# A decoder layer in float32: x transposed in blocks by VectorE and through DRAM, and an altered order of stages in the plan

## The chip, the cores and the metric

The kernel runs on one core of a Trainium2 chip. The core has a matrix engine (TensorE, PE in the profile, with its weight loads listed as PEld), a vector engine (VectorE, DVE), a scalar engine (ScalarE, ACT), GpSimd (POOL) and a queue engine (SyncE, SP) that issues transfers (DMAs). The engines run side by side and wait for one another by semaphores. The metric is the device time of one execution in microseconds (us), taken as the median of several runs.

## The reference

All data are float32. `x` has 16 batches of 512 tokens with 256 channels, and `ctx_1024` has 16 batches of 64 context tokens. Three sublayers follow one another, each added to its input and normalised over the channels:

```python
# 1. linear self-attention, 16 heads of 16 channels, K = 2
q  = x + x @ Wq + bq
ks = x + x @ Wk[k] + bk[k];  vs = x + x @ Wv[k] + bv[k]        # k = 0, 1
states[k] = einsum('bhnd,bhne->bhde', ks / 32, vs / 32)
out = einsum('bhnd,bhde->bhne', q, prod(states))               # no softmax
out = (layernorm(out) * ln_g + ln_b) @ Wo + bo
# 2. cross-attention to 64 context tokens, 16 heads of 64
out = softmax(q k^T * SCALE, masked) v @ Wout.T + b_out
# 3. mixture of experts: 8 experts, 256 -> 1024 -> 256, capacity 1024 tokens each
w = softmax(x @ router_w.T + router_b)
out[token] += w[token, e] * (relu(x[token] @ Wi[e]) @ Wo[e])   # first 1024 tokens with w > 0, per expert
```

With softmax weights nearly always above zero, each expert takes the first 1024 tokens, which are batches 0 and 1.

## The kernel before, in words

**Self-attention without ks and vs.** Because there is no softmax, the state of a batch needs only the Gram matrix of x (`x^T x`, 256x256) and the sums of x. `gram` (L550) loads x of one batch into `gx` with a column of ones (`load_gram_x`, L293: tokens on partitions, token t*128 + p in partition p), multiplies it with itself into `ps_g` and copies the result to `g`. The order of the tokens makes no difference to it. `self_attention` (L614) then multiplies `g` with the weights (`ps_gk` L629, `ps_s` L641), folds the state into one matrix `m` (`ps_m` L670), and applies it to x: `ps_o` (L687) needs x with channels on partitions, which is `xT`. Before the change `xT` is made from `xt`, a second load of x, by `transposed` (L227): per half of the channels four TensorE transposes of 128x128 into one PSUM bank (L233), and one copy out of it by `evac` (L182), in turn on ACT and DVE. Norm, a transpose of z (`zT`, which shares its one buffer with `xT`), the output product `ps_p` (L711), norm, and the transposed `x1T` follow.

**The other stages.** `context_keys` (L450), `output_weights` (L515) and `context_values` (L483) prepare keys and values of all batches once and store them in DRAM (`k_dram`, `vo_dram`). `cross_attention` (L765) per batch: a key product per pair of batches (`ps_kq` L751), scores `ps_sim` (L814), a softmax whose probabilities DVE transposes in 32x32 blocks (L804), and the product with the values `ps_x` (L834), for which `vo` comes from DRAM in 32 DMAs per batch. `routing` (L846) computes expert weights into `w_all`; the `experts` (L929, `ps_h` L946, `ps_e` L963) work on the first two batches, beside the attention of the others. `ranks` (L875) checks at the end whether later batches have tokens for an expert; the weights it lets through are written to `w_sel`, and a loop at the end of the kernel handles such batches. There are none here.

**The order.** The order of the instructions on PE, DVE, ACT and POOL is fixed by a planner: each stage is a generator, a `Stream`, that emits a few instructions at a time. `weave` (L1010) always advances the ready stream with the earliest planned time, where the time is that of `plan(at, span, total)`: start, length and PE work, so it moves on with the work done. `Model` (L28) estimates when each instruction would be done; `yield WAIT` makes a stream ready only when what it has emitted is done, `until(...)` waits for a condition. `in_order` (L1029) then ties the instructions of each of the four engines to that order. SP's queue, which issues all DMAs before the change, isn't tied by it. The constants are `SETUP = 115` and `STEP = 78` us, one step per batch. The Gram matrix of batch b >= 4 is planned at SETUP + (b - 4.8) STEP, the self-attention of b at SETUP + (b - 1) STEP, the cross-attention at SETUP + b STEP, routing one step later. The context stream (71 us of PE work, then 28 for the second half of the values) is planned from 5 us to about 200 us, and the experts from SETUP + 1.3 STEP on. The first four Gram matrices are planned within the first 40 us, and after the fourth the remaining weights are loaded.

## Time and profile before

| | us |
|---|---|
| median of 3 runs | 1384.72 (1383.49 to 1386.94) |
| the profiled execution | 1389.4 |
| its span | 1387.6 |
| granted TensorE clock, mean | 0.994 |
| DMA, share of 16 engines on SP's queue | 40.1% of the span, 151.98 MB |

The profile lists per engine the busy time in the span, then groups of instructions by source line: output tile, input tiles, shapes, count, busy time, mean time of one, and the idle time before them. A matmul in float32 is recorded as two instructions, a transpose as one. "L233" is line 233 of the kernel before. The chain follows the work that ended last backwards, always to what released it, so it tells what set the end. A table by stage gives the busy time of each engine in a stretch. In the middle of the run the steps of 78 us look alike.

### The profile page before, as it was taken

How to read it: one execution, taken by the hardware profiler on the slowest of the kernel's cores; microseconds unless marked ns; L12 is line 12 of the kernel's file. 1: busy time of each engine (PE TensorE's matmuls, PEld its weight loads, DVE VectorE, ACT ScalarE, POOL GpSimd, SP SyncE). 2: the span in 40 equal slices, each digit the busy share in tenths (PEclk: the TensorE clock that was granted, in tenths of full speed). 3: DMA queues.
4: the chain of work that ended last, by engine and by line, in shares of the span. 5: the costliest groups of instructions: out<-in, count | busy, mean ns of one | idle time of the engine just before them, and what ended most of it. 6: DMA issues, size and time to landing. Idle time of an engine off the chain costs nothing.

```text
span 1387.6 us, 24209 instructions
## 1 busy us (share of the span) xinstructions
PE 1365.9 (98%) x9630; PEld 1077.9 (78%) x9630; DVE 850.7 (61%) x1957; ACT 402.2 (29%) x912; POOL 203.7 (15%) x140
## 2 busy tenths in 40 slices
PE   8999999999999999999999999999999999999997
PEld 5766576877878787878878787878888787878686
DVE  2445848466584848475584848475665939484744
ACT  1134224132232314142233323142323323232322
POOL 0001112112020111112020112112020202111200
PEclk9999999999999999999999999999999999999999
DMA  8657775511515153522606053513334061505211
GB/s 260 203 136 191 189 195 163 142 32 42 145 53 150 46 142 106 127 77 52 181 24 164 31 142 106 126 62 77 110 95 123 16 187 46 147 26 126 91 56 40
DMA packets 98372, 153.57 MB, mean 111 GB/s; under 512 B 15560, under 2 KB 70096, under 8 KB 98256
## 3 DMA queue, kind: packets, MB, share of 16 engines
q1 hardware_dynamic: 98256, 151.98, 40.1%
q8 instruction: 78, 1.28, 0.4%
q14 instruction: 38, 0.31, 0.1%
HBM read 114.71 MB, written 37.22 MB: 109 GB/s over the span
## 4 chain that ended last, share of the span: by engine, by line
PE 89%; DVE 5%; DMA 2%; SPq 1%; ACT 1%; issue 1%; ACTq 0%; DVEq 0%
PE ps_x L834 16%; PE ps_sim L814 15%; PE ps_e L963 15%; PE ps_h L946 15%; PE ps_gk L629 4%; PE ps_p L711 4%; PE ps_o L687 3%; PE ps_kv L437 3%; PE ps_t L233 2%; PE ps_kq L751 2%; PE ps_vo L492 2%; PE ps_s L641 2%; PE ps_g L555 2%; PE ps_zt L700 1%; PE ps_m L670 1%; PE ps_g L560 1%
## 5 line engine op out<-in xcount | busy, mean ns | idle before, releaser
L946 PE MATMUL ps_h<-head_T,wi 128*128 128x256 f32 x1024 | 239.1, 379 | 0.0
L834 PE MATMUL ps_x<-vo,pT 32*128 32x264 f32 x4096 | 234.9, 384 | 3.9 <-DVE pT L804 3.7
L814 PE MATMUL ps_sim<-kq,x1T 128*128 128x512 f32 x512 | 235.0, 593 | 0.0
L834 PEld LDWEIGHTS ps_x<-vo,pT 32*128 32x128 f32 x4096 | 211.5, 186 | 26.1 <-issue 5.6
L946 PEld LDWEIGHTS ps_h<-head_T,wi 128*128 128x128 f32 x1024 | 193.4, 190 | 38.8 <-issue 13.0
L802 POOL TENSOR_TENSOR s<-s,sm 128x1024 f32<-128x1024 f32 x64 | 121.7, 1901 | 539.8 <-DVE sm L801 501.4
L841 DVE TENSOR_TENSOR x<-ps_x,x 128x264 f32<-128x264 f32 x64 | 23.2, 426 | 226.3 <-PE ps_x L834 226.3
L822 ACT ACTIVATE s<-s 128x512 f32<-128x512 f32 x128 | 80.7, 630 | 276.1 <-DVE s L821 276.0
L814 PEld LDWEIGHTS ps_sim<-kq,x1T 128*128 128x128 f32 x512 | 94.5, 190 | 83.2 <-issue 74.5
L820 DVE TENSOR_REDUCE mx<-ps_sim 128x8 f32<-128x512 f32 x128 | 86.1, 673 | 42.0 <-PE ps_sim L814 41.6
L821 DVE TENSOR_TENSOR s<-ps_sim,mx 128x512 f32<-128x512 f32 x128 | 88.5, 692 | 4.4
L725 POOL TENSOR_TENSOR x<-x,bout 128x1056 f32<-128x1056 f32 x16 | 38.7, 2420 | 320.7 <-ACT hT L952 172.6
L804 DVE STREAM_TRANSPOSE pT<-s 128x1024 f32<-128x1024 f32 x64 | 78.6, 1228 | 7.0 <-POOL s L802 7.0
L952 ACT ACTIVATE hT<-ps_h 128x256 f32<-128x256 f32 x128 | 46.9, 376 | 119.9 <-PE ps_h L946 119.8
L701 ACT ACTIVATE zT<-ps_zt,shift,gain 128x512 f32<-128x512 f32 x32 | 23.2, 775 | 189.5 <-PE ps_zt L700 189.5
L800 DVE TENSOR_REDUCE sm<-s 128x16 f32<-128x1024 f32 x64 | 77.1, 1204 | 0.4 <-ACT s L822 0.4
L261 ACT ACTIVATE rstd<-bn_mv,eps 128x4 f32<-128x4 f32 (+1 forms) x70 | 20.7, 295 | 159.5 <-DVE bn_mv L250 156.0
L267 ACT ACTIVATE x<-x,off,rstd 128x264 f32<-128x264 f32 (+1 forms) x112 | 58.3, 591 | 29.3 <-DVE off L265 29.3
L687 PE MATMUL ps_o<-m,xT 128*128 128x264 f32 x256 | 66.7, 387 | 0.0
L954 DVE TENSOR_SCALAR hT<-ps_h 128x256 f32<-128x256 f32 x128 | 52.2, 409 | 22.5 <-PE ps_h L946 22.3
L711 PE MATMUL ps_p<-wo,zT 128*128 128x264 f32 x256 | 63.1, 387 | 0.0
L629 PE MATMUL ps_gk<-wk,g 128*128 128x256 f32 x256 | 61.2, 382 | 0.0
(174 smaller groups left out, 1897.4 us busy)
## 6 DMA issues: line engine op xcount, KB each, us to landing
vo<-vo_dram SPq DMA_DIRECT2D x512, 132.0 KB, 4.2
vo_dram<-vst SPq DMA_DIRECT2D x128, 132.0 KB, 2.4
xt<-in_x_dram SPq DMA_DIRECT2D x16, 512.0 KB, 4.0
wi<-L_ffn_experts_inter_dram SPq DMA_DIRECT2D x8, 1024.0 KB, 5.3
gx<-in_x_dram SPq DMA_DIRECT2D x15, 512.0 KB, 4.2
x_rest<-x SPq DMA_DIRECT2D x14, 512.0 KB, 3.1
out_dram<-x SPq DMA_DIRECT2D x14, 512.0 KB, 2.9
kT<-k_dram SPq DMA_DIRECT2D x8, 512.0 KB, 3.3
```

The source lines that it names most:

```text
L629: nc.tensor.matmul(ps[:, :C], blk, wk[:, j, k, :], start=(j == 0), stop=(j == NC - 1))
L687: nc.tensor.matmul(ps[:, :CX], xT[:, cc, t * P:(t + 1) * P], m[:, cc, :], start=(cc == 0), stop=(cc == NC - 1))
L711: nc.tensor.matmul(ps[:, :CX], zT[:, cc, t * P:(t + 1) * P], wo[:, cc, :], start=(cc == 0), stop=(cc == NC - 1))
L802: nc.gpsimd.tensor_mul(s, s, sm.unsqueeze(2).to_broadcast([P, NH, J]))
L804: nc.vector.transpose(probsT[:, :, t, :], s.rearrange("p h (a j) -> p (h a) j", a=2))
L814: nc.tensor.matmul(ps, x1T[:, cc, t * P:(t + 1) * P], kq[:, cc, hf * 512:(hf + 1) * 512], start=(cc == 0), stop=(cc == NC - 1),)
L820: nc.vector.tensor_reduce(mx[:, hs], sim, AX.X, ALU.max)
L821: nc.vector.tensor_sub(s[:, hs, :], sim, mx[:, hs].unsqueeze(2).to_broadcast([P, 8, J]))
L822: nc.scalar.activation(s[:, hs, :], s[:, hs, :], AF.Exp, scale=SCALE)
L834: nc.tensor.matmul(ps[q][:, :CX], probsT[pq, blk].rearrange("p t i -> p (t i)"), vos[c][pq, i, :], start=(c == 0 and i == 0), stop=(c == 7 ...
L946: nc.tensor.matmul(ps[:, :TB], wi[:, cc, f * P:(f + 1) * P], head_T[b][:, cc, t0 * P:t0 * P + TB], start=(cc == 0), stop=(cc == NC - 1),)
L963: nc.tensor.matmul(ps[:, :C], hT[f][:, t * P:(t + 1) * P], wo_[:, f, :], start=(f == 0), stop=(f == NF - 1),)
```

## The change

For batches 1 to 15, TensorE no longer transposes x. `load_gram_x` loads `gx` in four DMAs of 32 partitions each, so that partition 32 i + j holds the tokens 128 i + 32 q + j. After the Gram matrix, `to_blocks` lets DVE transpose `gx` in 32x32 blocks (four instructions per batch) into `xb`. ACT's queue writes `xb` to a DRAM tile of the batch, `x_blocks`. At the start of the batch's self-attention, `from_blocks` reads it back in four DMAs on ACT's queue, each to 32 partitions of `xT`, where the blocks now stand as the full transpose. The layout of `xT` changes accordingly. Batch 0 still uses TensorE. The second load of x, `xt`, stays for the residual. The next `gx` is loaded after this instead of right after the Gram products, and the self-attention waits until its blocks are in DRAM, and before `ps_o` until `xT` is there.

In the plan, the first self-attention and the first cross-attention get the planned time 0, which makes them the most urgent whenever they are ready, and the later self-attentions move from b - 1 to b - 1.6 steps. The planner's model learns DMAs on ACT. `w_sel` is gone: `ranks` writes the weights of the later batches over `w_all`. Two small tiles keep one buffer.

```diff
@@ Model.run @@
-            if kind == "InstDMACopy":
+            if kind == "InstDMACopy" and engine == "Activation":
+                start = max(at, self.free.get(engine, 0.0))
+                self.free[engine] = start + 0.35
+                done = start + 5.0
+            elif kind == "InstDMACopy":
...
+                by = "SP" if kind == "InstDMACopy" else engine
+                self.used[n] = max(self.used.get(n, (0.0, None)), (done, by), key=lambda p: p[0])
...
@@ decoder_layer @@
-    w_sel = const.tile([P, NTT, E], FP, tag="w_sel", name="w_sel")
...
+    def to_blocks(src):
+        xb = wk1.tile([P, NT, NC, NT, 32], FP, tag="xb", name="xb")
+        for q in range(NT):
+            nc.vector.transpose(
+                xb[:, :, :, q, :].rearrange("p k c j -> p c k j"),
+                src[:, q, :C].rearrange("p (c k j) -> p c k j", c=NC, j=32),
+            )
+        return xb
+
+    def from_blocks(dst, there):
+        for k in range(NT):
+            nc.scalar.dma_start(
+                out=dst[k * 32:(k + 1) * 32].rearrange("i t c n -> i t (c n)"),
+                in_=there[:, :, k, :].rearrange("t i n -> i t n"),
+            )
...
-        def load_gram_x(b, eng=nc.sync, pieces=1):
+        def load_gram_x(b, eng=nc.sync, pieces=NT):
...
+                else:
+                    eng.dma_start(
+                        out=t[i * 32:(i + 1) * 32, :, :C],
+                        in_=x[b, i * P:(i + 1) * P, :].rearrange("(q j) c -> j q c", j=32),
+                    )
...
@@ gram @@
-            if b + 2 < B:
-                gram_x[b + 2] = load_gram_x(b + 2)
...
             grams[b] = g
+            if b > 0:
+                yield WAIT
+                xb = to_blocks(gx)
+                yield WAIT
+                x_blocks[b] = dram.tile([NT, 32, NT, NC * P], FP, tag=f"x_blocks{b}", name="x_blocks")
+                nc.scalar.dma_start(
+                    out=x_blocks[b].rearrange("t i k n -> (t i) (k n)"), in_=xb.rearrange("p k c q j -> p (k c q j)")
+                )
+            if b + 2 < B:
+                gram_x[b + 2] = load_gram_x(b + 2)
             yield WAIT
...
@@ self_attention @@
-            xT = wk1.tile([P, NC, S], FP, tag="xT", name="xT")
-            gks = []
+            xT = wk1.tile([P, NT, NC, P], FP, tag="xT", name="xT")
+            if b > 0:
+                from_blocks(xT, x_blocks.pop(b))
...
-            yield from until(lambda: made(xt))
-            transposed(xT, xt)
+            if b == 0:
+                yield from until(lambda: made(xt))
+                transposed(xT.rearrange("p t c n -> p c t n"), xt, lambda t: t)
             yield WAIT
...
+            yield from until(lambda: made(xT))
             z = wk1.tile([P, NT, CX], FP, tag="z", name="z")
...
-                        ps[:, :CX], xT[:, cc, t * P:(t + 1) * P], m[:, cc, :], start=(cc == 0), stop=(cc == NC - 1)
+                        ps[:, :CX], xT[:, t, cc], m[:, cc, :], start=(cc == 0), stop=(cc == NC - 1)
...
@@ ranks @@
-            nc.vector.scalar_tensor_tensor(w_sel, rank, float(CAP), w_all, ALU.is_lt, ALU.mult)
+            rest = slice(HEAD_B * NT, NTT)
+            nc.vector.scalar_tensor_tensor(
+                w_all[:, rest], rank[:, rest], float(CAP), w_all[:, rest], ALU.is_lt, ALU.mult
+            )
...
@@ all_self_attention @@
-                self_st.plan(SETUP + (b - 1) * STEP, STEP, 16.5)
-                yield from until(lambda: b in grams and sums[b // QB][1] and "rb" in cs and made(grams[b], sums[b // QB][1][0]))
+                if b > 0:
+                    self_st.plan(SETUP + (b - 1.6) * STEP, STEP, 16.5)
+                yield from until(
+                    lambda: b in grams and sums[b // QB][1] and "rb" in cs and made(grams[b], sums[b // QB][1][0])
+                    and (b == 0 or b in x_blocks and made(x_blocks[b]))
+                )
...
@@ all_cross_attention @@
-                cross_st.plan(SETUP + b * STEP, STEP, 28.2 + (0 if b % GB else 4.0))
+                if b > 0:
+                    cross_st.plan(SETUP + b * STEP, STEP, 28.2 + (0 if b % GB else 4.0))
...
-        self_st.plan(0.0, SETUP, 16.5)
-        cross_st.plan(SETUP, STEP, 28.0)
+        self_st.plan(0.0, 0.0, 1.0)
+        cross_st.plan(0.0, 0.0, 1.0)
```

More of the change, by code (lines that the diff above doesn't have):

```diff
@@ L98, in run @@
             for n in names[0] + names[1]:
-                self.used[n] = max(self.used.get(n, (0.0, None)), (done, engine), key=lambda p: p[0])
+                by = "SP" if kind == "InstDMACopy" else engine
+                self.used[n] = max(self.used.get(n, (0.0, None)), (done, by), key=lambda p: p[0])
             for n in names[1]:
-                self.made[n] = (done, engine)
+                self.made[n] = (done, "SP" if kind == "InstDMACopy" else engine)
         self.seen, self.end = len(traced), end
@@ L234, in transposed @@
             v = view(dst[:, cc, :])
-            ps = ps if len(v.shape) == 2 else ps.rearrange("p (q t i) -> p q t i", q=NT, t=NT)
+            if len(v.shape) > 2:
+                ps = ps.rearrange("p (q n) -> p q n", n=P) if len(v.shape) == 3 else ps.rearrange(
+                    "p (q t i) -> p q t i", q=NT, t=NT
+                )
             if ones and cc == NC - 1:
@@ L298, in load_gram_x @@
             for i in range(pieces):
-                eng.dma_start(
-                    out=t[:, i * n_:(i + 1) * n_, :C],
-                    in_=x[b, i * n_ * P:(i + 1) * n_ * P, :].rearrange("(t p) c -> p t c", p=P),
-                )
+                if b == 0:
+                    eng.dma_start(
+                        out=t[:, i * n_:(i + 1) * n_, :C],
+                        in_=x[b, i * n_ * P:(i + 1) * n_ * P, :].rearrange("(t p) c -> p t c", p=P),
+                    )
+                else:
+                    eng.dma_start(
+                        out=t[i * 32:(i + 1) * 32, :, :C],
+                        in_=x[b, i * P:(i + 1) * P, :].rearrange("(q j) c -> j q c", j=32),
+                    )
             return t
@@ L475, in context_keys @@
             nc.sync.dma_start(out=xwq, in_=x_wq.rearrange("(r p) c -> p r c", p=P))
-            last = small.tile([P, NP], FP, tag="last", name="last")
+            last = small.tile([P, NP], FP, tag="last", name="last", bufs=1)
             nc.vector.tensor_copy(last, xwq[:, :, C - 1])
@@ L605, in grams_of @@
                     yield WAIT
-        grams, sums = {}, {}
+        grams, sums, x_blocks = {}, {}, {}
         def load_x(b):
@@ L662, in self_attention @@
             nc.vector.scalar_tensor_tensor(state, state, STATE_SCALE, headmask, ALU.mult, ALU.mult)
-            yield from until(lambda: made(xt))
-            transposed(xT, xt)
+            if b == 0:
+                yield from until(lambda: made(xt))
+                transposed(xT.rearrange("p t c n -> p c t n"), xt, lambda t: t)
             yield WAIT
@@ L909, in ranks @@
             nc.vector.tensor_add(rank, rank, start)
-            nc.vector.scalar_tensor_tensor(w_sel, rank, float(CAP), w_all, ALU.is_lt, ALU.mult)
+            rest = slice(HEAD_B * NT, NTT)
+            nc.vector.scalar_tensor_tensor(
+                w_all[:, rest], rank[:, rest], float(CAP), w_all[:, rest], ALU.is_lt, ALU.mult
+            )
             NB = B - HEAD_B
-            least = small.tile([P, NB], FP, tag="least", name="least")
+            least = small.tile([P, NB], FP, tag="least", name="least", bufs=1)
             nc.vector.tensor_reduce(
@@ L1070, in all_self_attention @@
             for b in range(B):
-                self_st.plan(SETUP + (b - 1) * STEP, STEP, 16.5)
-                yield from until(lambda: b in grams and sums[b // QB][1] and "rb" in cs and made(grams[b], sums[b // QB][1][0]))
+                if b > 0:
[3 more added lines that the diff above has]
+                    and (b == 0 or b in x_blocks and made(x_blocks[b]))
+                )
                 yield from self_attention(b, done)
@@ L1163, in decoder_layer @@
         wb = fw.tile([P, NT, E], FP, tag="wb", name="wb")
-        nc.vector.tensor_copy(wb, w_sel[:, ds(i * NT + HEAD_B * NT, NT), :])
+        nc.vector.tensor_copy(wb, w_all[:, ds(i * NT + HEAD_B * NT, NT), :])
         aT = fw.tile([P, NC, S], FP, tag="aT", name="aT")
```

## The prediction

> **What bounds the kernel now.** I read the page's busy shares and its 40 slices first, then the busy time by stage, then the chain of work in a middle step, then the rows of the tiles that the change touches, and last the DMA issues of the set-up.
>
> ```profile
> span 1387.6 us, 24209 instructions
> PE 1365.9 (98%) x9630; PEld 1077.9 (78%) x9630; DVE 850.7 (61%) x1957; ACT 402.2 (29%) x912; POOL 203.7 (15%) x140
> ...
> PE   8999999999999999999999999999999999999997
> ```
>
> TensorE (PE) is busy 98% of the span. A busy PE need not be at its peak, so the stages come next (start and end in us, length, busy time of PE, PEld, DVE, ACT and POOL with their instruction counts, clock, DMA share, GB/s).
>
> ```profile
> 0.00:20.00 20.00, 13.90 (x61) 11.27 (x62) 4.09 (x15) 3.90 (x7) 2.25 (x14) 0.91 0.79 251
> 20.00:40.00 20.00, 20.00 (x71) 11.31 (x70) 5.45 (x13) 3.20 (x7) 0.10 (x1) 1.00 0.94 258
> 40.00:60.00 20.00, 20.00 (x87) 12.79 (x86) 7.47 (x20) 3.59 (x7) 0.10 (x1) 1.00 0.91 273
> ...
> 586.00:664.00 78.00, 78.00 (x594) 63.21 (x593) 49.33 (x114) 22.28 (x52) 12.60 (x8) 1.00 0.31 82
> ...
> 330.00:335.00 5.00, 3.57 (x17) 2.81 (x16) 4.75 (x15) 2.34 (x7) 1.50 (x1) 1.00 0.00 2
> 335.00:340.00 5.00, 3.18 (x32) 2.85 (x36) 1.67 (x2) 0.46 (x1) 2.85 (x3) 0.66 0.01 3
> ```
>
> From 352 us to 1288 us PE has no idle time worth counting. Its 21.7 us of idle are 6.1 us in the first 20 us, 6.3 us after 1381 us (last norm and store), 3.25 us at 333.5 us, where PE waits for a softmax transpose while DVE is 4.75 us busy of 5, 2.1 us at 1350 to 1366 us (ranks), and some 4 us in small pieces, most of them between 105 and 270 us. So in the middle PE work taken away is time won. The chain of a middle step (start, length, what):
>
> ```profile
> 620.72 1.73 PE ps_e L963 x8
> 622.45 0.87 PE ps_t L233 x8
> 623.32 1.72 PE ps_sim L814 x4
> ```
>
> It is PE from end to end, and L233's eight transposes of x into xT take 0.87 us of it (109 ns each, though a record says 272 ns, because they are pipelined). The rows of what is replaced, and the nearest row to what is added:
>
> ```profile
> L233 PE MATMUL ps_t<-ident,xt x128: 272/273/273, 62.6 to 1231.5; 128*128 128x128 f32 x128
> L186 ACT COPY xT<-ps_t x16: 562/567/588, 63.2 to 1231.7; 128x512 f32<-128x512 f32 x16
> L188 DVE COPY xT<-ps_t x16: 678/684/685, 64.3 to 1232.3; 128x512 f32<-128x512 f32 x16
> ...
> L804 DVE STREAM_TRANSPOSE pT<-s 128x1024 f32<-128x1024 f32 x64 | 78.6, 1228 | 7.0 <-POOL s L802 7.0
> ```
>
> And what one DMA issue costs the queue that makes it, quiet (18.60) and while the DMA engines are full (40.85, three of them):
>
> ```profile
> 18.60 0.37 SPq L299 DMA_DIRECT2D gx<-in_x_dram  x1
> ...
> 40.85 4.05 SPq L470 DMA_DIRECT2D k_dram<-stk  x3
> 45.01 1.38 SPq L299 DMA_DIRECT2D gx<-in_x_dram  x1
> ```
>
> **The change, part by part.**
>
> *Transposes leave PE.* Batches 1 to 15 lose eight transposes each: 15 x 0.87 = **-13.1 us**, all on the bounding engine. Their two copies out of PSUM (0.57 us ACT, 0.68 us DVE) go too, and two bank uses.
>
> *Blocks on DVE.* to_blocks adds four transposes of 128x256 per batch. The trace has only 128x1024 (1228 ns). DVE's slope from its reduces, 673 ns for 512 columns and 1204 ns for 1024, is 1.04 ns a column, so 1228 - 768 x 1.04 = 0.43 us; a quarter of the row, 0.31 us, is the other end. I take 0.43, since small DVE operations carry a fixed part: 1.7 us per batch, net +1.05 us after the copy that goes. DVE goes from 49.3 to about 50.4 us in a 78 us step, 62% of the span. Cost on the path: 0, covered by the PE work of the other streams. Without that cover, 15 x 1.05 = 16 us.
>
> Here a rule speaks against the change. The Trainium skill, "VectorE: DVE Perf Modes", The three transpose paths and Rules for kernel authors, gives 390 ns on TensorE and 311 ns on VectorE for a 128x128 bf16 transpose, says that VectorE does 32x32 blocks only, and advises TensorE where PSUM will do. By it nothing is won: near-equal price, plus a round trip; about 1385 us. The trace's row charges PE 109 ns per transpose in sequence, on the one engine without slack, while DVE has 38% idle. I go by the row.
>
> *ACT issues DMAs.* Per batch one write of 512 KB (xb to x_blocks) and four reads of 128 KB into xT, all on ACT's queue. By the issue rows that is 5 x 0.37 = 1.9 us on a quiet system and 5 x 1.36 = 6.8 us on a full one. I take 2.2 us, near the quiet end, because the DMA share of the middle steps is 0.28 to 0.46. ACT is 22.3 us busy of 78 in a step, and evictions behind the issue (hT, exp, kq copies) come 1 to 2 us later; eight PSUM banks at 0.86 us of PE each, and the other streams' work, cover that. On the path: 0. The price without cover is in the rivals. The write waits for DVE's blocks, but the plan yields before issuing it. The reads wait for that write, some three steps older (gram of b is planned at b-4.8 steps, self-attention at b-1.6), and for zT of the batch before, which is used up. xT is needed at ps_o: in the step shown gk starts at 601.0 and ps_o at 633.1 us, against landings of 4.2 us (vo<-vo_dram, 132 KB). So the new wait for xT costs 0.
>
> *DMA volume.* 15 x 1.05 MB = 15.7 MB on 153.6; the share rises from 40% to about 44%. Hidden in the middle. In the set-up three writes, 1.57 MB, join a share of 0.94; at 265 GB/s they are 5.9 us of transfer. PE is 20.00 of 20.00 busy there, so it isn't waiting for loads: between 0 and 5.9 us, taken **+1.0**.
>
> *gx in four pieces.* For b >= 1 SP issues four DMAs instead of one: 3 x 0.42 = 1.3 us more. For gx of batch 1 this stands, at 4.1 us, ahead of wk, bk and the first nat; PE idles 2.4 us for nat at 15.1 us. 0 to 1.5, taken **+1.0**. The skill's "DMA: Bandwidth & Descriptors", Rules for kernel authors, also speaks against splitting by partitions: both parts use the same engines, so one 128-partition transfer serves. By it the price is only the issues, as I count; the trace's pieces of 128 KB land in 2.2 us, the whole in 4.2. The later loads, which now stand behind the blocks and the ACT issue, have a step or more to spare; in the set-up gx of batch 3 comes later (issued at 18.6 us now), so key sums, self-attention of batch 0 and its weights may slip by 5 us or so. The context stream, 71 us of planned PE work, fills that.
>
> *The plan.* Batch 0's self- and cross-attention become the most urgent; self-attentions of b >= 1 move 0.6 x 78 = 47 us ahead. With each moves 16.5 us of PE, some 14 us of DVE, the 512 KB load of xt on SP and four ACT reads; with cross 0 its kT, mask and vo loads. No PE work goes away, so only idle can change: the 3.25 us stall at 333.5 us and the half clock after it (3.4 us at 0.5, 1.7 us lost), plus the 4 us of pieces, make at most 9 us to be won. Against it, batch 0's work is a filler used up early, and DVE, at 1.57 us per us of PE in the scores (5.4 us of DVE to 3.43 of ps_sim), meets the context copies earlier. Ends -9 and +7; taken **-2.5**, under a third of what is there, since the stall comes from self-attention 2, softmax 1 and routing falling together on DVE, which the move pulls apart.
>
> *w_sel gone, bufs=1.* A 0.69 us operation is shorter by an eighth, and two small tiles lose spare buffers; 0.
>
> Sum: 1387.6 - 13.1 + 1.0 + 1.0 - 2.5 = 1374.0 us of span. The profiled execution took 1389.4, that is 1.8 around the span, and lies 4.7 above the median 1384.7: 1374.0 + 1.8 - 4.7 = **1371 us**.
>
> **Rivals.**
> *ACT's issues are exposed (slower).* Place: the four reads at the start of each self-attention. The plan fixes ACT's order, so hT, exp and zT queue behind them, and PE behind hT. Price: at the full-system 6.8 us, with half of it exposed, 15 x 3.4 = 51 us; at 2.2 us with all of it exposed, 33 us (1371 + 33 = 1404). It decides from 0.9 us per batch exposed (no gain), 1.2 for slower. For it: two rows show 1.35 us per issue under load, and vo loads come 32 per batch. Against: ACT's idle gaps, and low DMA shares. About 1397, halfway.
> *The set-up loses.* All of the 5.9 us, 1.5 at the start, and filler missing once before the experts begin: 1387.6 - 13.1 + 5.9 + 1.5 = 1381.9 of span, 1379 with nothing from the plan.
> *DVE becomes the late engine.* Stalls like that at 333.5 us in several steps; four at 3.25 us eat the gain: 1384. For it: 4.75 of 5 us there. Against: 49.3 of 78 in the middle and no stall there.
> *The plan wins all its idle.* 9 us instead of 2.5 and no set-up loss: 1387.6 - 13.1 - 9 = 1365.5 of span, 1363.
> That the transposes were hidden anyway is excluded by the chain.
>
> **How the numbers follow.** Forecast 1371 with 0.60, its own range 1365 to 1378; plan wins all 0.08; set-up loses 0.12; DVE late 0.06; ACT exposed 0.14. 0.3%, about what this measurement tells from no change, is 4.2 us. Faster 0.60 + 0.08 + 0.12 = 0.80, same 0.06, slower 0.14. The range 1362 to 1384 leaves out the slower case and little else.
>
> **What would show it.** ps_t<-ident,xt x8 (from x128); DVE block transposes near 0.43 us, x60; PE busy near 1353 us, and still 78 of 78 in middle steps; ACT issues near 0.45 us each; no PE wait on xT; no stall near 333 us. The forecast is wrong if PE waits on ACT (hT, zT, s) at self-attention starts, if middle steps show PE below 77.5, or if PE idles over 5 us between 60 and 220 us.

## The result and the profile after

The changed kernel takes 1399.28 us (median of 4 runs, 1398.22 to 1401.29), the kernel before 1385.83 us beside it (4 runs, 1383.49 to 1387.24). The ratio is 1.010, 95% interval 1.008 to 1.0121: the change costs 13.5 us, where 13.7 us of gain had been forecast. Line numbers below are those of the changed kernel: `ps_t` is L237, `ps_g` L589, `ps_x` L879, `ps_h` L994, `to_blocks` L257, `from_blocks` L265.

First the page after: span and busy shares, ACT's DMA queue (packets, MB, share of the 16 engines), and the shares of the chain.

```profile
span 1398.2 us, 24169 instructions
PE 1355.1 (97%) x9510; PEld 1064.3 (76%) x9510; DVE 837.7 (60%) x2002; ACT 389.9 (28%) x897; POOL 203.4 (15%) x140
...
q10 hardware_dynamic: 10800, 15.73, 3.7%
...
PE 84%; DVE 8%; DMA 4%; SPq 2%; ACT 1%; issue 1%; POOL 0%; DVEq 0%; ACTq 0%; POOLq 0%
```

On the chain PE's share fell (89% before), and DVE's and DMA's rose (5% and 2% before): waits take a larger part of it. The transposes did leave PE: its busy time fell by 10.8 us (1365.9 to 1355.1). But the span grew by 10.6 us, so PE's idle time grew by 21.4 us, from 21.7 to 43.1. Where, the busy time by stretch tells (start and end, length, PE, PEld, DVE, ACT, POOL with instruction counts, clock, DMA share, GB/s). The kernel before, cut at the same places as the one after:

```profile
0.00:60.00 60.00, 53.90 (x215) 35.37 (x216) 17.01 (x48) 10.70 (x21) 2.46 (x16) 0.97 0.88 261
60.00:80.00 20.00, 20.00 (x121) 16.88 (x122) 9.60 (x23) 3.34 (x7) 0.00 (x0) 0.83 0.06 23
80.00:352.00 272.00, 265.27 (x1888) 195.65 (x1888) 165.38 (x367) 84.98 (x199) 40.24 (x27) 0.99 0.56 143
352.00:1366.00 1014.00, 1011.45 (x7350) 816.85 (x7343) 653.43 (x1504) 298.02 (x673) 161.01 (x97) 1.00 0.35 97
```

And the changed kernel, with one middle step of 78 us at the end:

```profile
0.00:60.00 60.00, 51.87 (x198) 32.25 (x198) 17.19 (x52) 10.19 (x19) 2.47 (x16) 0.97 0.79 225
60.00:80.00 20.00, 14.70 (x96) 13.38 (x95) 11.00 (x33) 2.62 (x5) 0.23 (x2) 0.91 0.66 207
80.00:352.00 272.00, 255.37 (x1646) 183.42 (x1644) 167.26 (x373) 84.81 (x198) 38.17 (x24) 0.99 0.57 143
352.00:1366.00 1014.00, 1008.90 (x7463) 814.55 (x7464) 629.37 (x1508) 284.21 (x652) 162.57 (x99) 1.00 0.41 110
...
586.00:664.00 78.00, 78.00 (x590) 63.12 (x589) 47.44 (x116) 22.93 (x53) 8.27 (x6) 1.00 0.37 98
```

Idle of PE is length less busy. Up to 80 us it rose from 6.1 to 13.4 us, from 80 to 352 us from 6.7 to 16.6, from 352 to 1366 us from 2.55 to 5.1, and in the tail by 1.6. So 17 of the 21 us were lost in the first quarter. The middle step is still PE from end to end. Whether the change wins there can't be read from how late one stage ends, because the plan moved the stages against each other: by the last `ps_h` of the first expert the changed kernel is 17.9 us late, by its last `ps_e` 11.0 us. The experiments below tell.

The single waits of PE (total, times, longest) have no large one among them:

```profile
PE ps_x L879 <- DMA vo<-vo_dram: 5.0, 2, 3.8
PE ps_x L879 <- DVE pT L849: 4.5, 2, 3.0
PE ps_g L589 <- DMA gx<-in_x_dram: 4.2, 2, 2.9
PE ps_t L237 <- DMA xt<-in_x_dram: 3.4, 1, 3.4
PE ps_p L756 <- ACT zT L746: 2.8, 2, 2.0
...
PE ps_wT L424 <- DVE early L353: 1.8, 1, 1.8
```

Three of them can be followed to their cause in the trace.

**The weights came late (60 to 80 us).** SP's queue in the set-up, in order of issue:

```profile
44.85 1.80 SPq L333 DMA_DIRECT2D gx<-in_x_dram  x3
...
52.73 1.92 SPq L333 DMA_DIRECT2D gx<-in_x_dram  x3
...
57.28 0.45 SPq L394 DMA_DIRECT2D early<-in_L_attn_Wq_dram  x1
...
63.58 0.51 SPq L653 DMA_DIRECT2D xt<-in_x_dram  x1
```

The same two issues in the kernel before:

```profile
29.07 0.43 SPq L360 DMA_DIRECT2D early<-in_L_attn_Wq_dram  x1
...
38.28 0.43 SPq L611 DMA_DIRECT2D xt<-in_x_dram  x1
```

So `early` (Wq) and `xt` of batch 0 are issued 25 to 28 us later. The weights are loaded after the fourth Gram matrix, and its `gx` now waits until the blocks of an earlier batch are made, and takes four issues instead of one. PE then stands for both:

```profile
62.02 0.66 PE L424 MATMUL ps_wT<-ident,early 128*128 128x128 f32 x4 [1.78 <-DVE early L353]
...
68.78 1.97 PE L237 MATMUL ps_t<-ident,xt 128*128 128x128 f32 x8 [3.35 <-DMA xt<-in_x_dram]
```

**Values that are still being stored (163 us).** SP's queue, and PE behind it, in the two views of the timeline:

```profile
148.79 11.57 SPq L531 DMA_DIRECT2D vo_dram<-vst  x16
160.41 11.20 SPq L826 DMA_DIRECT2D vo<-vo_dram  x23
```

```profile
163.06 10.70 PE L879 MATMUL ps_x<-vo,pT 32*128 32x264 f32 x132 [3.76 <-DMA vo<-vo_dram]
```

The cross-attention of batch 0 now comes 25 us earlier (its `ps_x` ends at 179.2 instead of 204.1 us), at a time when the values of other batches are still being stored. Its loads stand behind those 16 stores on SP.

**DVE in front of batch 1's ps_x (273 us).** DVE, POOL and PE in the timeline:

```profile
267.54 1.94 DVE L903 TENSOR_TENSOR w_all<-x_head,rb 128x32 f32<-128x32 f32 x1
...
269.73 0.19 DVE L905 TENSOR_TENSOR w_all<-w_all,rm 128x32 f32<-128x32 f32 x1
...
270.75 1.42 DVE L257 STREAM_TRANSPOSE xb<-gx 128x256 f32<-128x256 f32 x4
272.09 0.12 DVE L292 SCALAR_TENSOR_TENSOR off<-bn_mv,rstd 128x4 f32<-128x4 f32 x1
272.13 1.23 DVE L849 STREAM_TRANSPOSE pT<-s 128x1024 f32<-128x1024 f32 x1
```

```profile
267.52 1.91 POOL L847 TENSOR_TENSOR s<-s,sm 128x1024 f32<-128x1024 f32 x1 [3.17 <-DVE sm L846]
```

```profile
273.42 16.05 PE L879 MATMUL ps_x<-vo,pT 32*128 32x264 f32 x256 [3.01 <-DVE pT L849]
```

The transpose of the softmax that PE waits for stands behind 1.42 us of block transposes, and behind a 128x32 operation that took 1.94 us and ended with POOL's operation; in the kernel before its like took 0.16 us at 331.10 us, where POOL was not at work. Together that is 1.42 + 1.78 = 3.2 us of DVE. But the transpose also needs POOL's result, which was there at 269.43 us. By this estimate it would have started 2.7 us earlier without the two, which is most of the wait of 3.01 us.

### The profile page after: what moved, and what is told of

It is laid out like the page before. It is cut to its first block, busy times and chain, and to the rows that moved or that the text cites. A ratio compares the mean times of both kernels' runs of the same rounds, so it can differ in the third digit from the quotient of the medians.

```text
span 1398.2 us, 24169 instructions
## 1 busy us (share of the span) xinstructions
PE 1355.1 (97%) x9510; PEld 1064.3 (76%) x9510; DVE 837.7 (60%) x2002; ACT 389.9 (28%) x897; POOL 203.4 (15%) x140
## 4 chain that ended last, share of the span: by engine, by line
PE 84%; DVE 8%; DMA 4%; SPq 2%; ACT 1%; issue 1%; POOL 0%; DVEq 0%; ACTq 0%; POOLq 0%
PE ps_x L879 16%; PE ps_e L1011 15%; PE ps_h L994 14%; PE ps_sim L859 13%; PE ps_o L732 4%; PE ps_p L756 4%; PE ps_gk L672 3%; PE ps_kv L471 3%; PE ps_kq L796 2%; PE ps_s L684 2%; PE ps_g L589 1%; PE ps_t L237 1%; DMA vo_dram<-vst 1%; SPq L531 1%; PE ps_m L714 1%
## 5 line engine op out<-in xcount | busy, mean ns | idle before, releaser
L879 PE MATMUL ps_x<-vo,pT 32*128 32x264 f32 x4096 | 238.6, 387 | 9.5 <-DMA vo<-vo_dram 5.0
L994 PE MATMUL ps_h<-head_T,wi 128*128 128x256 f32 x1024 | 240.0, 380 | 0.1
L879 PEld LDWEIGHTS ps_x<-vo,pT 32*128 32x128 f32 x4096 | 212.6, 187 | 34.2 <-DMA vo<-vo_dram 7.0
L994 PEld LDWEIGHTS ps_h<-head_T,wi 128*128 128x128 f32 x1024 | 192.0, 190 | 46.3 <-issue 18.2
L886 DVE TENSOR_TENSOR x<-ps_x,x 128x264 f32<-128x264 f32 x64 | 23.2, 424 | 239.0 <-PE ps_x L879 239.0
L471 PE MATMUL ps_kv<-cT,wT 128*128 128x512 f32 x128 | 60.5, 610 | 2.0 <-ACT vst L191 2.0
L732 PE MATMUL ps_o<-m,xT 128*128 128x264 f32 x256 | 62.2, 389 | 0.0
L756 PEld LDWEIGHTS ps_p<-wo,zT 128*128 128x128 f32 x256 | 48.1, 190 | 13.4 <-ACT zT L746 4.8
```

The lines of the kernel that those rows point to most:

```text
L471: nc.tensor.matmul(ps, wT[:, cc, r % 4 * P:(r % 4 + 1) * P], cT[:, cc, q * 512:(q + 1) * 512], start=(cc == 0), stop=(cc == NC - 1),)
L732: nc.tensor.matmul(ps[:, :CX], xT[:, t, cc], m[:, cc, :], start=(cc == 0), stop=(cc == NC - 1))
L756: nc.tensor.matmul(ps[:, :CX], zT[:, cc, t * P:(t + 1) * P], wo[:, cc, :], start=(cc == 0), stop=(cc == NC - 1))
L879: nc.tensor.matmul(ps[q][:, :CX], probsT[pq, blk].rearrange("p t i -> p (t i)"), vos[c][pq, i, :], start=(c == 0 and i == 0), stop=(c == 7 ...
L994: nc.tensor.matmul(ps[:, :TB], wi[:, cc, f * P:(f + 1) * P], head_T[b][:, cc, t0 * P:t0 * P + TB], start=(cc == 0), stop=(cc == NC - 1),)
```

## The experiments

Each is compared with the kernel before on the same chip. "Idle" is PE's idle time up to 80 us / from 80 to 352 us / from 352 to 1366 us, from one profiled execution; in the kernel before it is 6.1 / 6.7 / 2.55.

### The three parts of the change, alone and in pairs

The blocks (with all that belongs to them, the planner's model too), the first batch ahead in the plan, and the self-attentions moved from b - 1 to b - 1.6 can be had in any combination.

Blocks alone, the plan as before:

```diff
-        self_st.plan(0.0, 0.0, 1.0)
-        cross_st.plan(0.0, 0.0, 1.0)
+        self_st.plan(0.0, SETUP, 16.5)
+        cross_st.plan(SETUP, STEP, 28.0)
...
-                if b > 0:
-                    self_st.plan(SETUP + (b - 1.6) * STEP, STEP, 16.5)
+                self_st.plan(SETUP + (b - 1) * STEP, STEP, 16.5)
...
-                if b > 0:
-                    cross_st.plan(SETUP + b * STEP, STEP, 28.2 + (0 if b % GB else 4.0))
+                cross_st.plan(SETUP + b * STEP, STEP, 28.2 + (0 if b % GB else 4.0))
```

> The blocks for batches 1 to 15, with the plan of before (first batch not ahead, self-attentions at b - 1). Theory A (the set-up loses because the later and split gx loads stand ahead of the remaining weights in SP's queue: those are issued at 31 to 63 us after the change, at 23 to 38 us before): most of the loss stays, so 1385 to 1395 us, the weights still issued after 50 us, and PE idle in the first 352 us well above the 12.8 us of before. Theory B (the loss is the plan: batch 0 ahead of all, then waits for vo and DVE at 160 to 300 us): 1370 to 1376 us, idle near 13 us.

Measured 1405.71 us, ratio 1.0136 (1.0108 to 1.0165): more than either theory had. Both plan parts without blocks are the same lines put the other way round into the kernel before:

> The kernel before with only the new plan (first self- and cross-attention at time 0, self-attentions at b - 1.6), with all transposes on PE and the old gx loads. Theory A: 1382 to 1388 us, the plan by itself is near neutral. Theory B: 1395 to 1405 us, PE waits for vo at the first ps_x and for pT near 270 us as in the changed kernel.

Measured 1407.49 us, ratio 1.0151 (1.0132 to 1.0169), just above the range of Theory B. Only the first batch ahead, in the kernel before:

```diff
-        self_st.plan(0.0, SETUP, 16.5)
-        cross_st.plan(SETUP, STEP, 28.0)
+        self_st.plan(0.0, 0.0, 1.0)
+        cross_st.plan(0.0, 0.0, 1.0)
...
-                self_st.plan(SETUP + (b - 1) * STEP, STEP, 16.5)
+                if b > 0:
+                    self_st.plan(SETUP + (b - 1) * STEP, STEP, 16.5)
...
-                cross_st.plan(SETUP + b * STEP, STEP, 28.2 + (0 if b % GB else 4.0))
+                if b > 0:
+                    cross_st.plan(SETUP + b * STEP, STEP, 28.2 + (0 if b % GB else 4.0))
```

> The kernel before with only the first self- and cross-attention at planned time 0 and the others as before. The whole new plan alone took 1407 us. If this half is what costs (xt, then vo, come too late for a batch that is hurried): 1398 to 1410 us. If the moved self-attentions cost: 1383 to 1390 us.

Measured 1413.08 us, ratio 1.0193 (1.0176 to 1.021). Only the self-attentions moved, in the kernel before:

```diff
-                self_st.plan(SETUP + (b - 1) * STEP, STEP, 16.5)
+                self_st.plan(SETUP + (b - 1.6 if b > 0 else b - 1) * STEP, STEP, 16.5)
```

> The kernel before with only the self-attentions of batches 1 to 15 planned 0.6 steps earlier. If the hurried first batch is the cause of the plan's loss: 1383 to 1390 us. If the moved self-attentions are: 1395 us or more, with PE waiting for off, for x (ACT) and for pT before 400 us.

Measured 1394.09 us, ratio 1.0056 (1.0034 to 1.0078). The changed kernel with its first batch back in its old place:

```diff
-        self_st.plan(0.0, 0.0, 1.0)
-        cross_st.plan(0.0, 0.0, 1.0)
+        self_st.plan(0.0, SETUP, 16.5)
+        cross_st.plan(SETUP, STEP, 28.0)
...
-                if b > 0:
-                    self_st.plan(SETUP + (b - 1.6) * STEP, STEP, 16.5)
+                self_st.plan(SETUP + (b - 1.6 if b > 0 else b - 1) * STEP, STEP, 16.5)
...
-                if b > 0:
-                    cross_st.plan(SETUP + b * STEP, STEP, 28.2 + (0 if b % GB else 4.0))
+                cross_st.plan(SETUP + b * STEP, STEP, 28.2 + (0 if b % GB else 4.0))
```

> The changed kernel with its first batch put back to its old place in the plan (self-attention of batch 0 due over the set-up, its cross-attention over the following 78 us); blocks and the earlier self-attentions of the other batches stay. Measured before: blocks alone +20 us against the kernel before, the first batch ahead alone +26, the self-attentions moved alone +8, both plan parts together +21, all three +13.5. If the parts simply added, this would be about +28. Theory 1 (the first batch ahead is what costs, in the changed kernel too): +0 to +8 us, below the changed kernel. Theory 2 (each part makes another order of the set-up, and what a part costs depends on the other two): anything else; then above the changed kernel, +15 to +28, and the loss in the stretch 0 to 370 us again.

Measured 1395.97 us, ratio 1.0058 (1.004 to 1.0076). And the changed kernel with the self-attentions back:

```diff
-                    self_st.plan(SETUP + (b - 1.6) * STEP, STEP, 16.5)
+                    self_st.plan(SETUP + (b - 1) * STEP, STEP, 16.5)
```

> The changed kernel with the self-attentions of the batches from 1 on put back to their old place (one step ahead of their cross-attention instead of 1.6); blocks and the first batch ahead stay. Theory 1 (the first batch ahead costs by itself, 26 us, and blocks come on top): +25 to +45 us. Theory 2 (the parts do not add): +10 to +25 us, with the idle time of TensorE before 370 us between 25 and 45 us as against 12.8 in the kernel before.

Measured 1404.34 us, ratio 1.013 (1.0105 to 1.0155). Together:

| blocks | first batch ahead | self-attention at b - 1.6 | ratio | idle, us |
|---|---|---|---|---|
| no | no | no | 1 | 6.1 / 6.7 / 2.55 |
| yes | no | no | 1.0136 | 14.6 / 16.2 / 4.9 |
| no | yes | no | 1.0193 | 7.0 / 20.5 / 5.9 |
| no | no | yes | 1.0056 | 5.9 / 11.8 / 1.1 |
| yes | yes | no | 1.0130 | 11.5 / 20.5 / 3.7 |
| yes | no | yes | 1.0058 | 9.7 / 14.9 / 3.8 |
| no | yes | yes | 1.0151 | 7.5 / 16.4 / 3.3 |
| yes | yes | yes | 1.0100 | 13.4 / 16.6 / 5.1 |

Two things follow. Every one of the parts, taken alone, makes the kernel slower, and most of the idle time of PE that it adds lies before 352 us. And they don't add: 1.36 + 1.93 + 0.56 would be 3.9%, all three give 1.0%. Set against the pair that lacks it, the first batch ahead costs 0.42%, the blocks save 0.5% and the earlier self-attentions save 0.3%, which is not clear of the two intervals. Only the first batch ahead costs both alone and as the last one added. PE's wait for `vo`, 2.5 to 5.0 us in all, stands in the five kernels that have the first batch ahead, and in none of the others: this wait belongs to that part. It is a small share of what that part costs alone. The run without it kept to its first theory, at the upper edge (0.58% of 1387 us is 8 us); the run with it and without the earlier self-attentions, 18 us above, to the second.

Is the order of before a lucky one, that any touch of the plan would spoil?

```diff
-    SETUP, STEP = 115.0, 78.0
+    SETUP, STEP = 117.0, 78.0
```

> The kernel before with one planner constant altered: SETUP 117 instead of 115, no other edit and the same work. Theory O: another order, with 5 to 20 us more idle time in the first 350 us: 1390 to 1405 us. If the order of before is nothing special: 1383 to 1388 us.

Measured 1385.58 us, ratio 0.9994 (0.9983 to 1.0005), idle 7.1 / 6.6 / 2.55. So not every touch spoils it: the order changes in the set-up, and nothing is lost. But it changes little. PE's stages of the first 400 us follow one another nearly as before, while with the self-attentions moved they differ widely. Whether another order as good exists was not tried.

### Blocks for the later batches only

If the loss lies in the set-up, blocks should win where the set-up doesn't see them. Batches below n keep TensorE's transposes, whole loads of `gx` and the load at its old place:

```diff
-            if b > 0:
+            if b >= 4:
                 yield WAIT
                 xb = to_blocks(gx)
...
-            if b > 0:
+            if b >= 4:
                 from_blocks(xT, x_blocks.pop(b))
...
-            if b == 0:
+            if b < 4:
                 yield from until(lambda: made(xt))
                 transposed(xT.rearrange("p t c n -> p c t n"), xt, lambda t: t)
```

With the plan of before and n = 4:

> Blocks only for batches 4 to 15, whose Gram matrices come after the set-up loads; batches 0 to 3 as before, plan as before. Twelve batches x 0.87 us leave PE: if neither DVE nor the ACT issues cost anything in the middle, 1385.8 - 10.4 = 1375 us, and the weights are issued at 23 to 38 us again. If the blocks or the ACT issues cost PE in the middle steps, 1380 us or more.

Measured 1407.77 us, ratio 1.0156 (1.0132 to 1.018), idle 7.6 / 17.7 / 7.7. With the changed plan and n = 4:

> Blocks only for batches 4 to 15, with the new plan. Theory A: the set-up is mended, 1372 to 1380 us. Theory B: the plan's loss stays, 1388 to 1396 us.

Measured 1403.38 us, ratio 1.0121 (1.0103 to 1.0138), idle 5.2 / 18.6 / 4.4. The first missed its 1375 us by 33 us, the second came out above both theories. The late weights are mended in both (14.6 us of idle before 80 us with blocks from batch 1 became 7.6, and 13.4 with the changed plan became 5.2), so it is the block work of the first batches, with its later and split loads of `gx`, that had made them late. But nothing was won: the idle time stands between 80 and 352 us instead. With the plan of before and n = 8:

> The planner with the plan of before, blocks only for batches 8 to 15. The order is that of before up to the Gram matrix of batch 8, at some 350 us, and re-planned after it. Theory O in the form that only the set-up is sensitive: 1385.8 - 8 x 0.87 = 1379 us. If re-planning costs in the middle too, 1385 us or more. Theory D (stalls only where DVE is full, before 350 us): 1379 us as well.

Measured 1382.46 us, ratio 0.9956 (0.9938 to 0.9975), idle 6.8 / 6.7 / 4.4: faster than the kernel before by 0.44%, or 6.1 us of the 7 that eight batches should bring. Between n = 4 and n = 8 lies the loss. With n = 8 and SETUP 117:

> The planner's own order with the plan of before, blocks from batch 8 on, SETUP 117 instead of 115: meant as the best version. With SETUP 115 it measured 1382.5, ratio 0.9956; SETUP 117 alone made no difference (0.9994). If the win is the blocks' and not a lucky order: ratio 0.993 to 0.997. If it hangs on the order: above 0.998.

Measured 1383.25 us, ratio 0.9969 (0.9949 to 0.9989). The gain stands in this second, slightly different order too.

### The same with the order held

With blocks the planner chooses another order, so the runs above mix two causes. In the following kernels the planner's choices for the kernel before were recorded and are replayed one by one; the blocks are put in at the end of their Gram matrix. The shorter `ranks` and the smaller buffers of the changed kernel are in all of them; they were not tried apart, and the run from batch 8 carries them too.

```diff
         def weave():
-            model.run()
-            while streams:
...
+            for i in picks:
+                next(made_streams[i].gen, "end")
```

From batch 1, 4, 6, 7 and 8 on (in these kernels `to_blocks` is L263, `ps_x` L886, `ps_h` L1001):

> The same held order with blocks for batches 1 to 15. Theory O with the set-up's gx loads harmless: 1373 us. If the later and split gx loads hold up SP's queue also in the old order: PE waits between 20 and 80 us again by 6 to 8 us, 1379 to 1383 us. Theory D: over 1395 us.

> The order of the stages of the kernel before, held literally (the planner's picks are replayed), with blocks for batches 4 to 15 put in at the end of their Gram matrix. Theory O (what loses is the re-planned order: any change of the planner's costs or times gives another order in the set-up, with more idle time, while the blocks themselves are good): 1385.8 - 12 x 0.87 = 1375 us, 1372 to 1379. Theory D (the blocks' own DVE and ACT work stalls PE between 130 and 350 us, whatever the order): 1395 us or more.

> The held order with blocks for batches 6 to 15, so that no block is made or written before 235 us. If what loses lies in the stretch from 120 to 235 us (Gram matrices 4 and 5 between the vo traffic and the experts' first weights): 1385.8 - 10 x 0.87 + 2 us of idle seen in the middle = 1379 us. If the loss lies in the blocks wherever they stand: above 1387 us.

> The order of the kernel before held, blocks from batch 7 on: one batch more than the run with blocks from 8 (1380.9, ratio 0.9942), one less than the run with blocks from 6 (1390.2, ratio 1.0021). Theory A (it is batch 6's block work, which stands in the same microseconds as the last vst stores and the first head_T copy at 212 to 220 us, that costs the 10 us between those two): as with blocks from 8 or 0.8 us better, ratio 0.993 to 0.996, the first ps_h waits under 1 us and ps_x of batch 1 under 1 us. Theory B (batch 7's block work at about 250 us, at ps_x of batch 1, costs as much): ratio 0.998 to 1.002, ps_x of batch 1 waits 2 us or more.

> The order of the kernel before held instruction by instruction, blocks only for batches 8 to 15, so that no block's work falls before the first experts. Theory A (a batch with blocks wins 0.8 us of TensorE in the saturated middle, and loses only where set-up and first experts meet): 8 x 0.87 = -7.0 us of TensorE, less some 1 us of later waits: 1378 to 1381, and the first ps_h, ps_x of batch 1 and 2 wait as in the kernel before (0, 0.5, 3.3). Theory B (blocks cost their gain in later waits wherever they stand, with the order held): 1384 to 1388.

| blocks from | us | ratio | idle, us | PE waits longest at |
|---|---|---|---|---|
| 1 | 1406.32 | 1.0131 (1.0101 to 1.0162) | 11.3 / 13.7 / 6.7 | `wi` 5.2, `ps_x` of batch 2 4.5, `xt` 2.8 |
| 4 | 1396.78 | 1.0071 (1.0046 to 1.0097) | 7.3 / 15.8 / 3.3 | `ps_x` of batch 2 4.6, `wi` 2.6, `g` 2.6, `ps_x` of batch 1 2.5 |
| 6 | 1390.16 | 1.0021 (1.0007 to 1.0035) | 6.4 / 14.7 / 3.6 | `ps_x` of batch 2 4.6, first `ps_h` 3.6, `ps_x` of batch 1 2.5 |
| 7 | 1386.19 | 1.0011 (0.9991 to 1.003) | 6.0 / 10.7 / 3.6 | `ps_x` of batch 2 4.6, `ps_x` of batch 1 2.5 |
| 8 | 1380.87 | 0.9942 (0.9925 to 0.996) | 6.1 / 7.4 / 3.1 | `ps_x` of batch 2 3.3, as before |

The staircase shows the loss without the planner. Blocks in the seven batches whose block work falls before 352 us cost more than the 0.87 us of PE that each saves: going from 8 to 7, from 6 to 4 and from 4 to 1 costs 0.7, 0.5 and 0.6%, while the step from 7 to 6, 0.1%, is not clear of the intervals. The eight batches behind save theirs. With eight batches, 8 x 0.87 = 7.0 us are due, and the forecast of 1378 to 1381 us was met (1387.17 x 0.0058 = 8.0 us won, 5.5 to 10.4 by the interval). The run with blocks from 6 was expected at about 1379 and missed that by 11 us; the next lines explain part of that miss. The run from 7 was to tell whether batch 6 alone costs it, and says no: at 1.0011 it went the way of its Theory B, so batch 7's blocks already lose what the eight others win.

What the profiled executions show of the steps from 8 to 7 and from 7 to 6 can be read. DVE of the run with blocks from 7, then its POOL and its PE:

```profile
247.30 2.20 DVE L912 TENSOR_TENSOR w_all<-w_all,rm 128x32 f32<-128x32 f32 x1
...
330.69 1.41 DVE L263 STREAM_TRANSPOSE xb<-gx 128x256 f32<-128x256 f32 x4
```

```profile
247.11 2.35 POOL L757 TENSOR_TENSOR xt<-xt,bo 128x1024 f32<-128x1024 f32 x1
```

```profile
251.60 14.52 PE L886 MATMUL ps_x<-vo,pT 32*128 32x264 f32 x256 [2.48 <-DVE off L298]
...
336.98 17.19 PE L886 MATMUL ps_x<-vo,pT 32*128 32x264 f32 x256 [4.55 <-DVE pT L856]
```

And the same places of the run with blocks from 8, DVE, POOL and PE:

```profile
248.19 0.19 DVE L912 TENSOR_TENSOR w_all<-w_all,rm 128x32 f32<-128x32 f32 x1
```

```profile
248.33 0.10 POOL L330 MEMSET gx<- 128x4 f32 x1 [0.45 <-PE ps_g L602]
248.37 0.21 POOL L756 COPY xt<-z 128x32 f32<-128x32 f32 x1
248.54 2.35 POOL L757 TENSOR_TENSOR xt<-xt,bo 128x1024 f32<-128x1024 f32 x1
```

```profile
250.49 14.52 PE L886 MATMUL ps_x<-vo,pT 32*128 32x264 f32 x256 [0.50 <-DVE pT L856]
...
334.58 16.21 PE L886 MATMUL ps_x<-vo,pT 32*128 32x264 f32 x256 [3.26 <-DVE pT L856]
```

The blocks of batch 7 are made at 330.69 us, in front of a softmax that PE already waited for: 3.26 + 1.41 = 4.67 us, measured 4.55. And 80 us before that work, its mere place matters: with blocks the load of the next `gx`, and so POOL's memset of its column of ones, moves behind the blocks. Without the memset, which stood 0.45 us for `ps_g` and so held POOL back, POOL's `xt<-xt,bo` starts 1.4 us earlier (0.9 us of this is a lead that this execution has on DVE too), DVE's small `w_all` operation meets it and lasts 2.20 us instead of 0.19, until POOL's is over (249.46 us), and the `ps_x` of batch 1 waits 2.0 us longer. Both together are 3.3 us of PE, which is the difference in idle time from 80 to 352 us (10.7 against 7.4). The two ratios lie 0.7% apart, at least 0.3% by their intervals, that is 4 to 10 us. The two profiled executions lie only 2.6 us apart in span; they are the fastest of the ten with blocks from 7 and the slowest of the four from 8. The `ps_x` of batch 2 also runs 1.0 us longer behind its longer wait (17.19 against 16.21 us), with 6.8 us at half clock in the trace against 3.4. So these waits are part of the step, and the rest is not settled.

What the run from 6 adds in the trace is batch 6's block work at 212 us, next to the first expert. DVE and PE of the run with blocks from 6:

```profile
220.28 0.69 DVE L199 COPY head_T<-ps_t 128x512 f32<-128x512 f32 x1 [4.24 <-DMA gx<-in_x_dram]
```

```profile
227.75 1.16 PE L1001 MATMUL ps_h<-head_T,wi 128*128 128x256 f32 x4 [3.61 <-ACT s L874]
```

`head_T` is the first tile in memory that the set-up gives back, and its copies wait for transfers: in the kernel before DVE stood 0.22 us there for `vo_dram<-vst`. Now it stood 4.24 us, for a piece of `gx` by the trace, with softmax work behind it in its queue. The write of the blocks, 512 KB, goes out at 213.71 us among these stores. Held back behind the copy:

```diff
-                nc.scalar.dma_start(
-                    out=x_blocks[b].rearrange("t i k n -> (t i) (k n)"), in_=xb.rearrange("p k c q j -> p (k c q j)")
-                )
+                if b == 6:
+                    late.append(put)
+                else:
+                    put()
...
                 transposed(head_T[b], x2)
+                while late:
+                    late.pop()()
```

> As the run with the order held and blocks from batch 6 on, but the write of batch 6's blocks to DRAM is issued behind the first head_T copy instead of ahead of it. In that run VectorE and ScalarE stood for 4.24 and 3.41 us in front of this copy, which may only write when the last vst stores of the set-up have landed (its memory was theirs), and the first ps_h matmul then waited 3.61 us for the softmax, ps_x of batch 1 2.48 us. Theory A (the 512 KB block write shares the DMA engines with the last vst stores and makes them late): the copy's wait falls to 1.5 us or less, the ps_h wait to about 1, and the time from 1390.2 to 1384 to 1387. Theory B (the four gx pieces and the xt load at the same place, or something else, make it late): the wait stays at 3 us or more and the time at 1389 to 1392.

Measured 1390.36 us, ratio 1.0022 (1.001 to 1.0033): no gain that can be told from the 1.0021 with the write in its place. In the profiled execution DVE's wait fell from 4.24 to 2.70 us and that of `ps_h` from 3.61 to 2.01 us, but this execution was the fastest of twenty (1385.93 us), so it need not be the edit that shortened them. The time is as Theory B has it, the waits lie between the two: the write may be part of what makes the copy late, and is not all of it. The split `gx` load and `xt` at the same place are the other suspects; they were not tried apart.

One more suspect was ACT's queue. In the run with blocks from 4, a write of blocks stood still on it at 215.53 us until an unrelated `vo` load had landed, since in this program the DMAs of both queues share eight semaphores (the trace has eight, each taken in turn, and each DMA waits for the one before on its own). With the block DMAs on SP's queue instead, order held, blocks from 4:

```diff
-            nc.scalar.dma_start(
+            nc.sync.dma_start(
                 out=dst[k * 32:(k + 1) * 32].rearrange("i t c n -> i t (c n)"),
...
-                nc.scalar.dma_start(
+                nc.sync.dma_start(
                     out=x_blocks[b].rearrange("t i k n -> (t i) (k n)"), in_=xb.rearrange("p k c q j -> p (k c q j)")
```

> The held order with blocks for batches 4 to 15 (1396.8 us with ACT's queue), but x_blocks written and read on SP's queue. In the former the chain from 206 to 232 us runs over vo loads, ACT's write of x_blocks, DVE's next blocks, another write and wi. If ACT's standing still at its DMA issues (until an unrelated vo load has landed) is the cause: 1380 to 1388 us. If the cause is that two Gram matrices follow each other closely, with one xb buffer, or that wi comes late whatever the queue: 1393 us or more.

Measured 1396.6 us, ratio 1.0076 (1.0055 to 1.0096), against 1.0071 on ACT: that ACT stands at its DMA issues is not the cause. The eight semaphores are shared on SP's queue too, so what they cost is not excluded.

## Why the prediction was wrong, point by point

The forecast was 1374.0 us of span, and 1398.2 were measured. Of its sum, the PE work was to give -13.1 us and gave -10.8; all the rest, which is idle time of PE, was taken at +1.0 + 1.0 - 2.5 = -0.5 us and came to +21.4. So it is the idle time that the prediction had wrong, in three of its steps.

*What bounds the kernel* was read rightly: in the middle, PE work taken away is time won. *Transposes leave PE* was forecast at -13.1 us; the busy time of PE fell by 10.8 us, and the run with eight batches won what its eight were to give. *Blocks on DVE* were taken at 0.43 us each and measured 0.403; *ACT's issues* at 2.2 us per batch and measured about 2.1 (write 0.344, four reads of 0.442 in the median). The rows of the changed kernel (minimum, median, maximum in ns):

```profile
L237 PE MATMUL ps_t<-ident,xt x8: 421/421/475, 68.8 to 70.3; 128*128 128x128 f32 x8
...
L257 DVE STREAM_TRANSPOSE xb<-gx x60: 386/403/445, 30.5 to 1009.1; 128x256 f32<-128x256 f32 x60
...
L613 ACTq DMA_DIRECT2D x_blocks<-xb x15: 326/344/353, 31.9 to 1011.4; - x15
...
L265 ACTq DMA_DIRECT2D xT<-x_blocks x60: 309/442/1250, 106.0 to 1194.6; - x60
```

PE never waited for `xT`, as said. So the sum's prices of single operations held, and the row that it went by, 109 ns of PE per transpose, fits the gain of the run from 8.

**The step that failed first is *The plan*.** It was taken at -2.5 us between ends of -9 and +7, on the argument that no work goes away, that at most 9 us of idle time are to be won, and that the move pulls the stall at 333.5 us apart. Measured without blocks it costs 1.51%, 21 us, three times the worse end. The error was to count the idle time that is there, and not what a full pipeline loses when its start is put in another order. The upper end of +7 had no working behind it. The dearer of the two parts is the first batch ahead, 1.93% alone against 0.56% for the moved self-attentions: batch 0's loads come while the context stages still fill SP's queue (`vo` 3.76 us). That it is also missed later as filler was said in the prediction without a price, and no run shows it apart. The stall at 333.5 us was to be pulled apart; it is gone from there, and the changed kernel has waits of 3.01 us at 273, 2.16 us at 352.6 and 1.53 us at 358 us.

**The second is the 0 for DVE's blocks on the path,** "covered by the PE work of the other streams". The cover was taken from middle steps (49.3 of 78 us) and applied to all 15 batches. With the order held, blocks in the first seven of them cost what the staircase shows. In the kernel before, the profile lines at 330 us that the prediction itself shows have DVE at 4.75 of 5 us with PE waiting; there, with blocks from 7 and the order held, 1.41 us of blocks are 1.3 us of PE. Even a middle step shows it once: at 566.4 us of the changed kernel PE waits 1.97 us for ACT's `zT`, and ACT for DVE, which had done 1.43 us of blocks and two 128x32 operations of 0.84 and 2.21 us shortly before. The rival "DVE becomes the late engine" named this and was given 0.06, and counted four stalls of the old size, not the blocks' own length.

**The third is the set-up.** "Its weights may slip by 5 us or so" was 25 us, and "the context stream fills that" did not hold: PE lost 5.3 us between 60 and 80 us. The steps *DMA volume* and *gx in four pieces* put +2.0 us on it; the idle time up to 80 us grew by 7.3. The rival "the set-up loses" named the missing filler too, but its sum has no term for it. That PE was busy at a DMA share of 0.94 was read as proof that it doesn't wait for loads. It showed only that nothing that PE needed then was late; weights stood in the queue behind loads that the change made later.

The rival for the slower side, exposed issues of ACT, has nothing for it in the changed kernel's waits: the 1.97 us for `zT` lead back to DVE. Of the signs that were to prove the forecast wrong, "PE idles over 5 us between 60 and 220 us" came true: 13.6 us there, against 3.0 before.

What stays open is how the three parts combine. That the blocks cost 1.36% alone and save 0.5% beside the new plan was measured, but no run shows which of the many small waits goes away.

## What to carry to other kernels

A stage that is saturated in its middle can still be lost at its start: an edit should be priced separately for the stretch in which set-up, first use and steady state meet, with that stretch's own queues and its own late engine, and be left out there if it pays only later; here blocks from batch 8 on gain 0.3 to 0.6%, where blocks from batch 1 on lose 1.3 to 1.4%. A changed order of work is not bounded by the idle time that can be seen before it; if its upper end has no row behind it, it needs a wide one. When a planner reacts to an edit, hold its order to see what the edit alone does.

## What the runs showed of the hardware

A DVE operation with two inputs in SBUF that starts while POOL runs one lasts until POOL's is done: 128x32 elements in 2.20 instead of 0.19 us beside a POOL operation of 2.35 us, and 1.94 instead of 0.16 us beside one of 1.91 us. In the changed kernel ten of the two-input operations on `w_all` start under a two-input operation of POOL, and all ten end 0.05 us after it. One that started near the end of POOL's lost little, 0.24 us instead of 0.16; copies out of PSUM and 32x32 transposes of 128x1024 beside the same POOL operations kept their 0.42 and 1.23 us. The Trainium skill, "SBUF — State Buffer", section "SBUF: two separate sides", tells of such an exclusive lock for VectorE operations with two SBUF inputs, and the trace agrees. That a memset more or less on POOL decides whether the two meet, and so moves PE by 2 us, was read from the traces of two kernels, not tried apart.

Stalls of PE can cost more than their length, since the clock that it is granted falls behind many of them. The run with only the first batch ahead has the PE instructions of the kernel before, 9630. Its idle time of PE is 20.2 us longer, and its busy time 8.2 us longer as well (1374.1 against 1365.9): behind each of its stalls of 6.12, 6.75 and 5.50 us the trace has 6.8 us at half clock, and 38 us in all, against 17 us in the kernel before.

But the clock falls elsewhere too, and not alike in each execution. In the kernel before 6.8 us at half clock begin at 66.7 us, where PE is busy throughout (20.00 of 20.00 us at 0.83 in the table above) with transposes and 128x8 matmuls; what brings it down there isn't shown. The run with SETUP 117, with the same 9630 instructions, has 6.4 us at half clock and 1360.0 us of busy time. So the busy times of two single executions can differ by 6 us without any change of the work.
